# Fifteen products for eighteen in w1, and layernorm 1 of the next image by halves beside fc2

## The chip, the core and the metric

The kernel runs on one core of one Trainium2 chip. A core has a matrix engine (TensorE, PE in the profile), three engines for elementwise work (VectorE or DVE, ScalarE or ACT, GpSimd or POOL), a queue engine (SyncE or SP) and 16 DMA engines; they run side by side and wait for each other by semaphores. TensorE writes to PSUM banks (128 partitions by 512 float32), the others read them from there. The metric is the device time of one execution in microseconds, lower is better. Everything is computed in float32.

## The reference

Eight images of 384 channels by 32 by 32 pixels pass through a transformer block and then a ConvNeXt block. Cut to what matters here:

```python
# layer 0, per image, 1024 tokens of 384 channels
xn = layernorm(xf, g1, beta1)                       # layernorm 1
qkv = einsum('bnc,oc->bno', xn, w_qkv) + b_qkv
...                                                 # attention with 8 heads of 48, projection
x1 = out + shortcut
xn2 = layernorm(x1, g2, beta2)                      # layernorm 2
h = gelu(einsum('bnc,oc->bno', xn2, w_fc1) + b_fc1) # 384 -> 1536
y = x1 + einsum('bnh,oh->bno', h, w_fc2) + b_fc2    # 1536 -> 384
# layer 1
y = depthwise_conv7x7(x) + dw_b
y = layernorm(y) * ln_w + ln_b                      # layernorm 3
y = gelu(einsum('bhwc,cd->bhwd', y, w1) + b1)       # 384 -> 1536
gx = sqrt(sum(y * y, axis=(1, 2)))
y = grn_gamma * (y * gx / (mean(gx) + eps)) + grn_beta + y
y = einsum('bhwd,dc->bhwc', y, w2) + b2             # 1536 -> 384
out = x + y
```

## The kernel before

Channels lie on the partitions: an image is a tile of 128 partitions by 3 by 1024 (CT is 3, N is 1024, NH is 512, half an image). Images are counted from 0 to 7. A product is one matmul of a 128 by 128 block of weights with 512 tokens.

**Stages.** The loop at L1759 goes through the images. For image b it runs q and k, attention, fc1 for the first half of the tokens and then the second (`mlp`, L882), and fc2 (`by_thirds`, L908). Then it ends layer 1 of image b-1: w1 (`grn_up`, L1124), the values of image b+1 (`next_values`, L1730), w2 (`grn_down`). The depthwise convolution of image b runs on DVE beside these stages (`convolution`, L1061), with some taps made by ACT and added by POOL's DMA (`help_convolution`, L1092). Image 7 and the last layernorms have a path of their own.

**Fewer products.** fc2, w2 and q/k use a scheme in which a matrix cut in 3 by 3 blocks times one cut in 3 by 2 takes 15 products and not 18: some sums of the weight blocks are made once, in image 0, and kept in DRAM (`sums_singly`, L1370, for q/k), some sums of the token blocks are made for each image (`thirds_of`, L388), and the results are combined by DVE and ACT (`tiles_by_thirds`, L406, with the tables SINGLY, BANKS and SUMS). w1 uses another: for a pair of output tiles, 11 products instead of 12, with four differences of token blocks (`block_differences`, L1115) in the tile `attn` and weight sums in `s_w1`.

**The planner.** Work that is not TensorE's own is written as generators. `Flow` (L136) counts the products issued, each as 0.857 us; a generator says how long it wants to wait, and its next step is issued at the first product end after that. `after(first, chain)` asks every 1.0 us whether another chain has ended, `finish` issues the rest of a chain at once. The planner only decides in which order instructions stand in the five engines' programs; each engine then runs its own in order.

**Layernorms.** `layernorm` (L485) takes half an image: two adds over the three channel tiles (L499, L502), a sum over the partitions by TensorE, subtraction (L509), squares on ACT (L516), two adds (L520, L523), again a sum, Ln and Exp on ACT, and three multiplications (L537). Where a half is folded (`token_sums`, L459), POOL's DMA first adds one half of the partitions to the other (L474), and TensorE sums on one half of its rows only (L480):

```python
nc.gpsimd.dma_start(out=t[rows[j], cols], in_=t[rows[1 - j], cols], accum_op=ALU.add)
yield wait
...
for i in rows:
    nc.tensor.matmul(out=total[i, :], lhsT=ones[rows[j], :64], rhs=t[rows[j], cols], start=True, stop=True)
```

`abreast` (L549) runs the two halves of an image step by step beside each other, one folded to the upper rows and one to the lower. Layernorm 3 (`conv_norm`, L1696) and layernorm 1 of the next image (`next_norms`, L1706) are such pairs. The second comes 50 us after the end of fc1, behind layernorm 3; it falls into w1. The image for it is loaded at the end of fc1, because the tile `xn` has one buffer, which layernorm 2 also writes for fc1.

**Queues.** SP's queue holds the loads of weights (nine ring buffers, `Weights`, L283), of images and the small transfers of attention. POOL's holds the folds, the helped taps and the accumulating DMAs of fc2 and w2 (`adding`, L949, and `difference`, L866).

Of the kernel before, what the change touches and what calls it, by code (L numbers as in the profile page):

```python
# [51 lines left out]
P = 128  # L52
# [123 lines left out]
def block_kernel(  # L176
# [10 lines left out]
    w1: bass.AP,  # L187
    w2: bass.AP,
# [20 lines left out]
    s_w1 = dram.tile([P, HT // 2, 4, P], F32, tag="s_w1", bufs=1, name="s_w1")  # L209
# [7 lines left out]
    def load_x(b, tag, parts=2, engine=nc.sync):  # L217
        xt = one.tile([P, CT, N], F32, tag=tag, name=f"{tag}_{b}")
        src = image_of(x, b).rearrange("(c p) n -> p c n", p=P)
        for i in range(parts):  # L220
            cols = slice(i * N // parts, (i + 1) * N // parts)
            engine.dma_start(out=xt[:, :, cols], in_=src[:, :, cols])
        return xt

    vec = const.tile([P, NVEC], F32, name="vec")
    wqkv = const.tile([P, 3 * CT * C], F32, name="wqkv")
    wqk_sb = wqkv[:, : 2 * CT * C].rearrange("p (c m o) -> p c m o", c=CT, o=P)
    wv_sb = wqkv[:, 2 * CT * C :].rearrange("p (c o) -> p c o", c=CT)
    wproj_sb = const.tile([P, CT, C], F32, name="wproj_sb")
    ident = const.tile([P, P], F32, name="ident")  # L230
# [9 lines left out]
    third_e = const.tile([P, NH], F32, name="third_e")  # L240
# [112 lines left out]
    def plan_w1(tag, fast=True):  # L353
        plan = []
        for i in range(NC):
            plan.append(((f"w1_{tag}", i, "A"), chunk(w1, i)))
            if fast:
                plan.append(((f"w1_{tag}", i, "S"), s_w1[:, i, :, :].rearrange("p j o -> p (j o)")))
        return plan
# [28 lines left out]
    def thirds_of(src, places, e):  # L388

        b11, b12, b21, b22, b31, b32 = (src[:, s, half(n)] for s in range(CT) for n in range(2))  # L390
        f, h, e2, g, f2, h2, g2, f3, d = places
# [12 lines left out]
        return steps, (b12, b21, e, b22, f, h, e2, g, b31, f2, h2, g2, f3, b32, d)  # L404

# [138 lines left out]
    def weight_places(name):  # L544

        tiles = [three.tile([P, 2, NH], F32, tag="p", name=f"{name}_{i}") for i in range(2)]
        return [t[:, j, :] for t in tiles for j in range(2)]

# [30 lines left out]

    def qk(b, xn, weights=None):  # L580
# [3 lines left out]
        big = one.tile([P, HT * N], F32, tag="big", name=f"qk_{b}")  # L584
        parts = big[:, : 2 * NP * N].rearrange("p (i m n) -> p i m n", i=2, m=NP)
        if b == 0:
            spare_sums.append(big[:, 2 * NP * N :])
# [148 lines left out]
    def attention(b, xt, qT, kT, last_tile, ready, first):  # L736
# [44 lines left out]
        for n in range(len(steps) + 2):  # L781
# [10 lines left out]
            if n - 2 == len(steps) // 2 + 6:  # L792
                for chain in first:
                    flow.finish(chain)
                xn = one.tile([P, CT, N], F32, tag="xn", name=f"xn2_{b}")
# [20 lines left out]
    def exact_attention(xt, qT, kT):  # L816

        nc.vector.memset(attn, 0.0)
        for qt in range(N // P):
# [295 lines left out]
    def block_differences(acc):  # L1115

        b11, b12, b21, b22 = (acc[:, s, half(n)] for s in range(2) for n in range(2))
        t1, t2, t3, t4 = (attn[:, i, :] for i in range(4))
        yield 3.0
        for dst, one_, other in ((t1, b12, b11), (t2, b22, t1), (t3, b22, b12), (t4, b21, t2)):  # L1120
            nc.vector.tensor_tensor(dst, one_, other, ALU.subtract)
            yield 1.2

    def grn_up(b, acc, weights, tag):  # L1124
# [5 lines left out]
        b11, b12, b21, b22, b31, b32 = (acc[:, s, half(n)] for s in range(CT) for n in range(2))  # L1130
        t1, t2, t3, t4 = (attn[:, i, :] for i in range(4))
        wa = f"w1_{tag}"
        spent = {}

        def finish(m):
            other_table(y[:, m, :], y[:, m, :], AF.Gelu, bias=b1[:, m : m + 1])

        def squares(i):
            for m in (i, i + HT // 2):
                waste = spent[i].rearrange("p a n -> p (a n)")  # L1140
                nc.scalar.activation(waste, y[:, m, :], AF.Square, accum_out=gx[:, m : m + 1])

        for i in range(HT // 2):
            j = i + HT // 2
            raw, sums = weights.at(wa, i, "A"), weights.at(wa, i, "S")
            a11, a12, a13, a22, a23 = (raw[:, k, :] for k in range(5))
            s1, s2, s3, s4 = (sums[:, k, :] for k in range(4))
            spent[i] = ps_s.tile([P, 2, NH], F32, tag="s", name=f"h_{b}_{i}_5")
            p5 = spent[i][:, 0, :]
            c11, c12, c21, c22 = (y[:, m, half(n)] for m in (i, j) for n in range(2))  # L1150

            def product(*pairs):
                bank = o_tile(f"h_{b}_{i}")
                accumulate(bank, list(pairs))
                return bank

            def plus(dst, bank, part):
                nc.vector.tensor_tensor(dst, bank, part, ALU.add)  # L1158

            nc.scalar.copy(c21, product((a11, b11)))  # L1160
            if i:
                finish(j - 1)
                squares(i - 1)
            plus(c11, product((a13, b31), (a12, b21)), c21)
            accumulate(p5, [(s1, t1)])
            plus(c21, product((s2, t2)), c21)
            plus(c12, p5, c21)
            plus(c12, product((s4, b22), (a13, b32)), c12)
            finish(i)
            plus(c21, product((s3, t3)), c21)  # L1170
            plus(c22, p5, c21)
            plus(c21, product((a23, b31), (a22, t4)), c21)
# [791 lines left out]
```

## Time and profile before

| | us |
|---|---|
| three runs | 3286.0, 3287.73, 3288.41; median 3287.73 |
| the profiled execution | 3286.43, its span 3284.5 |
| granted TensorE clock, mean | 0.996 |
| start of fc2, w1 and values of image 3 | 1359.4, 1413.3, 1472.6 |

The page gives busy time of each engine over the whole span; its stages differ, so the parts are read from the order of time of one image. Lines that begin with a line number are groups of instructions: engine, operation, tiles, shapes, count, busy time and mean of one. A mean of 592 ns for a matmul of 512 columns is the length of one of its two passes, which overlap; the distance from one product to the next is what counts. Such rows of the page are:

```profile
L444 PE MATMUL h<-acc,w_A 128*128 128x512 f32 x432 | 207.4, 596 | 0.0
L1158 DVE TENSOR_TENSOR y<-h,y 128x512 f32<-128x512 f32 x288 | 198.1, 690 | 93.6 <-PE h L444 80.4
hid<-hid POOLq DMA_DIRECT2D x42, 512.0 KB, 7.9
```

The first is part of w1's products, in two passes each; the second the adds by which w1's results are combined, 48 for an image; the third the accumulating DMAs of fc2 with the median time from issue to landing.

### The profile page before, as it was taken

The page shows a single profiled execution, that of the slowest core. Times are in us where ns is not written, and L with a number is a line of the kernel's source. Part 1 is how long each engine was busy: PE and PEld are TensorE (multiplying, and loading weights), DVE is VectorE, ACT ScalarE, POOL GpSimd, SP SyncE. Part 2 cuts the span into 40 slices and gives each one's busy share as a digit, 9 for nine tenths or more (in the row PEclk, how much of TensorE's full clock was granted, in tenths as well). Part 3 has the DMA queues.
Part 4 walks back from the last instruction along what each step waited for, and adds up shares of the span by engine and source line. Part 5 has one row for each costly group of instructions (what it writes and reads, how often), then busy time and mean ns, then how long its engine had stood idle before and what let it go on. Part 6 is the DMA issues. An engine that isn't in the chain of part 4 may idle for free. (4 is left out here: it accounts for less than half of the span.)

```text
span 3284.5 us, 38862 instructions
## 1 busy us (share of the span) xinstructions
PE 3262.0 (99%) x14288; PEld 1410.0 (43%) x14288; DVE 2413.3 (73%) x3220; ACT 1630.0 (50%) x2243; POOL 481.8 (15%) x567
## 2 busy tenths in 40 slices
PE   9999999999999999999999999999999999999999
PEld 5334444443344434444334443444434444444455
DVE  4444787787867878678786787867887788879850
ACT  3542763447634375353762646526474365723631
POOL 2111210112110121101211012110221112200000
PEclk9999999999999999999999999999999999999999
DMA  6336733647345563536536374273843637433231
GB/s 236 115 109 146 166 61 78 154 111 171 60 97 144 135 139 58 127 116 169 102 61 140 106 188 82 56 169 87 202 74 61 179 88 189 74 79 85 68 91 54
DMA packets 202160, 380.08 MB, mean 116 GB/s; under 512 B 41072, under 2 KB 47088, under 8 KB 201328
## 3 DMA queue, kind: packets, MB, share of 16 engines
q0 software_dynamic: 80928, 161.78, 26.7%
q1 hardware_dynamic: 120752, 215.09, 21.3%
q8 instruction: 114, 1.87, 0.2%
q10 hardware_dynamic: 288, 0.71, 0.1%
q14 instruction: 78, 0.64, 0.1%
HBM read 197.25 MB, written 35.78 MB: 71 GB/s over the span
## 5 line engine op out<-in xcount | busy, mean ns | idle before, releaser
L1087 DVE SCALAR_TENSOR_TENSOR acc<-pad,vec,acc 128x870 f32<-128x870 f32 (+8 forms) x861 | 963.1, 1154 | 7.0 <-DMA acc<-tap 1.7
L756 ACT ACTIVATE p<-s 128x1024 f32<-128x1024 f32 x512 | 524.4, 1024 | 267.0 <-PE s L747 260.2
L747 PE MATMUL s<-qk 48*64 48x512 f32 x4096 | 537.9, 592 | 0.7 <-ACT qk L593 0.7
L767 PE MATMUL o<-p,v 64*64 64x512 f32 x4096 | 534.5, 589 | 0.0
L384 PE MATMUL fc<-xn,fc 128*128 128x512 f32 x1152 | 502.6, 595 | 2.0 <-DVE acc L509 2.0
L1109 POOL DMA_DIRECT2D acc<-tap x294 | 253.4, 868 | 1184.5 <-ACT tap L1108 698.6
L384 PEld LDWEIGHTS fc<-xn,fc 128*128 128x128 f32 x1152 | 218.6, 190 | 282.0 <-issue 271.6
L444 PE MATMUL fc_p<-hid,fc 128*128 128x512 f32 x728 | 319.3, 594 | 0.0
L456 ACT ACTIVATE hid<-fc,bfc_f 128x512 f32<-128x512 f32 x192 | 131.4, 686 | 339.8 <-PE fc L384 339.7
L767 PEld LDWEIGHTS o<-p,v 64*64 64x64 f32 x4096 | 162.2, 133 | 278.7 <-issue 272.8
L747 PEld LDWEIGHTS s<-qk 48*64 48x64 f32 x4096 | 158.4, 133 | 278.1 <-issue 225.9
L444 PE MATMUL o_p<-y,w 128*128 128x512 f32 x624 | 270.9, 592 | 0.0
L1158 DVE TENSOR_TENSOR y<-h,y 128x512 f32<-128x512 f32 x288 | 198.1, 690 | 93.6 <-PE h L444 80.4
L1108 ACT ACTIVATE tap<-pad,vec 128x512 f32<-128x512 f32 x294 | 215.9, 735 | 1.4 <-DMA acc<-tap 1.2
L444 PEld LDWEIGHTS fc_p<-hid,fc 128*128 128x128 f32 x728 | 137.4, 190 | 178.7 <-issue 174.9
L444 PE MATMUL h<-acc,w_A 128*128 128x512 f32 x432 | 207.4, 596 | 0.0
L444 PEld LDWEIGHTS o_p<-y,w 128*128 128x128 f32 x624 | 118.0, 190 | 148.7 <-issue 134.9
L1087 DVE SCALAR_TENSOR_TENSOR wqkv<-pad,vec,wqkv 128x377 f32<-128x377 f32 (+24 forms) x288 | 177.3, 686 | 0.6
L876 ACT COPY pad<-x 128x512 f32<-128x512 f32 x48 | 30.2, 635 | 253.6 <-DVE x L942 196.6
L708 DVE TENSOR_TENSOR attn<-o,attn 128x512 f32<-128x512 f32 x64 | 44.1, 689 | 152.1 <-ACT attn L706 152.1
L689 PE MATMUL proj<-attn,wproj_sb 128*128 128x512 f32 x288 | 127.3, 595 | 1.1 <-DVE attn L734 1.1
L444 PEld LDWEIGHTS h<-acc,w_A 128*128 128x128 f32 x432 | 80.6, 190 | 109.0 <-issue 93.4
(361 smaller groups left out, 3822.8 us busy)
## 6 DMA issues: line engine op xcount, KB each, us to landing
acc<-tap POOLq DMA_DIRECT2D x294, 256.0 KB, 3.6
w_A<-in_w SPq DMA_DIRECT2D x72, 384.0 KB, 3.3
fc<-s_fc SPq DMA_DIRECT2D x91, 256.0 KB, 4.3
hid<-hid POOLq DMA_DIRECT2D x42, 512.0 KB, 7.9
fc<-in_wfc SPq DMA_DIRECT2D x54, 384.0 KB, 4.2
w<-s_w SPq DMA_DIRECT2D x78, 256.0 KB, 2.6
y<-y POOLq DMA_DIRECT2D x36, 512.0 KB, 7.1
qk<-s_qk SPq DMA_DIRECT2D x42, 320.0 KB, 5.0
```

The lines of the kernel that those rows point to most:

```text
L384: nc.tensor.matmul(out=ps, lhsT=lhsT(k), rhs=rhs(k)[:, half(h)], start=(k == 0), stop=(k == nk - 1))
L444: nc.tensor.matmul(out=bank, lhsT=lhsT, rhs=rhs, start=k == 0, stop=k == len(pairs) - 1)
L456: nc.scalar.activation(dst, src, function, **kw)
L689: nc.tensor.matmul(out=ps, lhsT=wproj_sb[:, m, ct * P : (ct + 1) * P], rhs=attn[:, m, :], start=(m == 0), stop=(m == CT - 1),)
L708: nc.vector.tensor_tensor(attn[:, m, :], outs[1], attn[:, m, :], ALU.add)
L747: nc.tensor.matmul(out=s[64 * i : 64 * i + 64, j, :], lhsT=kT[64 * j : 64 * j + HD, m, k0 : k0 + 64], rhs=qT[64 * j : 64 * j + HD, m, half ...
L756: nc.scalar.activation(p, s, AF.Exp)
L767: nc.tensor.matmul(out=outs[i][64 * j : 64 * j + 64, :], lhsT=v[keys, t, at : at + 64], rhs=p[keys, j, :], start=(t == 0), stop=(t == KT - 1),
L1087: nc.vector.scalar_tensor_tensor(dst, window, tap, dst, ALU.mult, ALU.add)
L1108: nc.scalar.mul(t.rearrange("p (h w) -> p h w", w=W), window, tap)
L1109: nc.gpsimd.dma_start(out=acc[:, ct, half(h)], in_=t, accum_op=ALU.add)
L1158: nc.vector.tensor_tensor(dst, bank, part, ALU.add)
```

## The change

Five things are changed.

1. w1 is computed by `tiles_by_thirds`, in four groups of 15 products for 3 output tiles each. Its weight sums are made in image 0 from a new input `w1t`, with those of q/k, by two chains that go through one group at a time (`sums_for_tiles`), and its token sums by ten differences (`make_thirds`) in place of four.
2. The tile `xn` has two buffers. One takes the next image, loaded in the middle of attention (`next_image`); the other holds layernorm 2's output for fc1 and then six of the token sums, of w1 first and of q/k later (`before_fc2`).
3. From image 2 to image 6 the rest of the convolution is issued when layernorm 2 ends, and layernorm 3 starts 16 us later (`end_soon`).
4. Layernorm 1 of the next image no longer comes after layernorm 3 as a pair. Its halves run one after the other (`halves_of_next`), from 24 us after layernorm 2 (1 us in image 1), with the tiles `res` for their sums; in image 0 it stays a pair.
5. To make room, wqk no longer has a place of its own (it is loaded into the big tile of q and k), and `ident`, `third_e` and w1's old sums are gone; the last image's convolution is kept in an `xn` buffer.

```diff
-        xt = one.tile([P, CT, N], F32, tag=tag, name=f"{tag}_{b}")
+        xt = one.tile([P, CT, N], F32, tag=tag, bufs=2 if tag == "xn" else 1, name=f"{tag}_{b}")
...
-    def thirds_of(src, places, e):
+    def thirds_of(src, spare):
...
-        f, h, e2, g, f2, h2, g2, f3, d = places
+        f, h, e2, g = averages()
+        e, f2, h2, g2, f3, d = (spare[:, s, half(n)] for s in range(CT) for n in range(2))
...
+    def make_thirds(what, src, us, spare):
+        steps, thirds[what] = thirds_of(src, spare)
+        for step in steps:
+            nc.vector.tensor_tensor(*step)
+            yield us
...
+                next_image(b)
                 for m in (NP - 1, *range(CT)):
                     flow.finish(chains[0, m])
...
+        def gelu(g, r):
+            m = g + 4 * (r - 1)
             other_table(y[:, m, :], y[:, m, :], AF.Gelu, bias=b1[:, m : m + 1])
...
+        def square(g, r):
+            m = g + 4 * (r - 1)
+            nc.scalar.activation(waste, y[:, m, :], AF.Square, accum_out=gx[:, m : m + 1])
+
+        for g in range(HT // CT):
+            tiles = {}
...
+            def behind(n):
+                if g and n == 3:
+                    gelu(g - 1, 2)
+                    gelu(g - 1, 1)
+                elif g and n == 1:
+                    square(g - 1, 2)
+                elif g and n == 4:
+                    square(g - 1, 1)
+                elif n == 14:
+                    gelu(g, 3)
+                elif n == 7:
+                    square(g, 3)
+
+            c = {f"c{r + 1}{n + 1}": y[:, g + 4 * r, half(n)] for r in range(CT) for n in range(2)}
+            for _ in tiles_by_thirds(weights, f"w1_{tag}", g, thirds["w1"], c, bank, behind):
+                pass
+        for what in (gelu, square):
+            for r in (2, 1):
+                what(g, r)
...
         def conv_norm(b, ln):
-            if b > 0:
+            if b == 0:
+                xn = state["xn"]
+                norm = abreast(xn, xn, eps0, "g1", "ln1_1", True, gentle=True)
+                state["norm1"] = flow.spawn(after(ln, norm))
+            else:
                 acc = state["acc"]
                 how = dict(wait=5.0) if b < B - 1 else dict(wait=3.4, factor=2.4)
                 norm = abreast(acc, acc, eps1, "lnw", f"ln3_{b - 1}", True, **how)
-                if b < B - 1:
-                    norm = sequence(norm, block_differences(acc))
-                state["norm3"] = flow.spawn(after(ln, after(state["help"], after(state["conv"], norm))))
-
-        def next_norms(b):
+                if 1 < b < B - 1:
+                    state["norm3"] = flow.spawn(after(ln, sequence(end_soon(b), norm)))
+                    state["norm1"] = flow.spawn(after(ln, halves_of_next(b, 24.0)))
+                else:
+                    state["norm3"] = flow.spawn(after(ln, after(state["help"], after(state["conv"], norm))))
+                if b == 1:
+                    state["norm1"] = flow.spawn(after(ln, halves_of_next(b, 1.0)))
...
+        def sums_for_tiles(i):
+            width = len(FORMS) * P
+            spare = large[0][:, (2 * NP + 2 * i) * N : (2 * NP + 2 * i + 2) * N]
+            for w, store, g in ((wqkt, s_qk, i), (w1t, s_w1, i), (w1t, s_w1, i + 2)):
+                yield from sums_singly(w[:, g * width : (g + 1) * width], store[:, g : g + 1], spare)
+                yield 8.0
...
+        def end_soon(b):
+            end_convolution(b)
+            yield 16.0
...
+        def halves_of_next(b, us):
+            yield us
+            xn = state["xn"]
+            for h in range(2):
                 name = f"ln1_{b + 1}"
-                places = (lambda: weight_places(name)) if b else averages
-                norm = abreast(xn, xn, eps0, "g1", name, True, places=places, gentle=b > 0, factor=1.4 if b else 1.7)
-                state["norm1"] = flow.spawn(after(state["norm3"], norm, 50 if b else 11))
...
+                places = lambda: res_places(f"{name}_{h}")
+                yield from layernorm(xn, xn, h, eps0, "g1", name, True, spare=places, fold=h, wait=5.0, gentle=True)
+
+        def before_fc2(b):
+
+            end_convolution(b)
+            spare = state["spare"] = one.tile([P, CT, N], F32, tag="xn", bufs=2, name=f"thirds_{b}")
+            if b > 0:
+                state["w1"] = flow.spawn(after(state["norm3"], make_thirds("w1", state["acc"], 1.4, spare)))
...
             if b < B - 1:
-                y, gx = grn_up(b - 1, acc, weights, b - 1)
+                flow.finish(state["w1"])
+                flow.finish(state["norm1"])
+                y, gx = grn_up(b - 1, weights, b - 1)
```

## The prediction

> **What bounds the kernel now.** I read the page first (busy shares, slices), then TensorE's waits, then the order of time of one image (number 3 of 0 to 7, 1140 to 1538 us; numbers 2 to 6 repeat it with a period of 398 us), and last how long DMAs take to land.
>
> ```profile
> PE 3262.0 (99%) x14288; PEld 1410.0 (43%) x14288; DVE 2413.3 (73%) x3220; ACT 1630.0 (50%) x2243; POOL 481.8 (15%) x567
> DVE  4444787787867878678786787867887788879850
> ```
>
> TensorE (PE) is busy 99% of the span: what the change takes from it is time, and what it makes it wait is time. VectorE (DVE) is at 73%, but unevenly. Of the waits of PE two rows matter:
>
> ```profile
> PE ln_var L480 <- DMA ln_sq<-ln_sq: 2.5, 3, 1.3
> PE ln_sum L480 <- DMA ln_a<-ln_a: 1.9, 1, 1.9
> ```
>
> So 4.4 us go to folded layernorm sums whose DMA was late, all in the first two images; from 900 to 2800 us PE waits 1.1 us in all, and for no fold. What a product and a sum cost is read from the w1 stage in PE's order of time (start, length, instructions):
>
> ```profile
> 1419.32 1.02 PE L444 MATMUL h<-attn,w_S 128*128 128x512 f32 x2
> 1420.17 1.02 PE L444 MATMUL h<-acc,w_A 128*128 128x512 f32 x2
> 1421.03 1.02 PE L444 MATMUL h<-attn,w_A 128*128 128x512 f32 x2
> 1421.98 0.65 PE L480 MATMUL ln_sum<-ln_a,ones 64*64 64x512 f32 x2
> 1422.00 0.65 PE L480 MATMUL ln_sum<-ln,ones 64*64 64x512 f32 x2
> 1422.46 0.59 PE L480 MATMUL ln_sum<-ln_a,ones 64*64 64x512 f32 x2
> 1422.48 0.60 PE L480 MATMUL ln_sum<-ln,ones 64*64 64x512 f32 x2
> 1423.00 3.89 PE L444 MATMUL h<-acc,w_A 128*128 128x512 f32 x8
> ```
>
> From start to start a product takes 0.858 us (the groups' mean of 1.02 counts an overlap). The sums of *both* halves of layernorm 1 run beside each other, on different quarters of the array: 1423.00 - 1421.03 - 0.86 = 1.11 us for the two together.
>
> In fc2 of this image (1359.4 to 1413.3) DVE runs in bursts:
>
> ```profile
> 1386.72 2.35 DVE L942 TENSOR_TENSOR hid<-hid 128x1024 f32<-128x1024 f32 x2
> 1388.99 0.74 DVE L939 SCALAR_TENSOR_TENSOR x<-fc_p,vec,x 128x512 f32<-128x512 f32 x1
> 1389.65 0.74 DVE L939 SCALAR_TENSOR_TENSOR x<-fc_n,vec,x 128x512 f32<-128x512 f32 x1
> 1390.31 0.68 DVE L942 TENSOR_TENSOR fc_spare<-fc_n,fc_spare 128x512 f32<-128x512 f32 x1
> 1391.03 0.69 DVE L942 TENSOR_TENSOR x<-fc_spare,x 128x512 f32<-128x512 f32 x1
> 1391.63 0.68 DVE L942 TENSOR_TENSOR fc_spare<-fc_spare 128x512 f32<-128x512 f32 x1
> 1392.35 0.69 DVE L942 TENSOR_TENSOR x<-fc_spare,x 128x512 f32<-128x512 f32 x1
> ```
>
> This is what is issued at once after the seventh of the fifteen products of fc2 (four matmuls each): 6.9 us with the add before it (1386.1 to 1393.0), in which nothing else gets through. A fold in its turn is a 128 KB accumulating DMA on POOL. Behind two 512 KB ones of fc2 (image 1, issues from 581 to 587 us; then image 3, where nothing was ahead of it):
>
> ```profile
> hid<-hid POOLq DMA_DIRECT2D x2, 512.0 KB, 7.8
> ln_sq<-ln_sq POOLq DMA_DIRECT2D x1, 128.0 KB, 9.4
> attn<-attn POOLq DMA_DIRECT2D x1, 128.0 KB, 9.8
> ```
> ```profile
> ln_sq<-ln_sq POOLq DMA_DIRECT2D x1, 128.0 KB, 3.7
> ```
>
> 9.4 us against 3.7 from issue to landing. The reader should keep three things: PE full, DVE lumpy in fc2, a fold slow behind the adds.
>
> [...]
>
> **The change part by part.** The working is against the profiled run, 3286.43 us (span 3284.5 and 1.9 around it, 1.3 under the median of 3287.73).
>
> *w1.* Six images (0 to 5) go through it. Before: six pairs of 11 matmuls, 66; after: four groups of 15, 60. 36 matmuls by 0.858 = **-30.9 us**. Their rate stays 0.858 if DVE and ACT keep up. The same form runs in q/k without a wait of PE. For w1, by slots of 0.858 (a group is 12.9): DVE has 11 adds of 0.63 to 0.69, 7.6 us; ACT 5 copies of 0.58, 3 gelus of 1.05 to 1.15 and 3 squares of 1.2, 9.9 us. The tightest return is bank n: slot 12's two subtractions end at 12.6, the next group wants it at 12.9. Slot 5 wants the add of slot 2 (ends 3.4, wanted 4.3); slot 8 the copy of slot 5 (5.9, wanted 6.9). Taken at nothing; if 0.5 us per group is lost, +12. Weights are 12 loads of 320 KB for 6 of 384 and 6 of 256: 3.84 MB both times. The tail on ACT is two gelus and two squares for one and two: about 0.5 us later at a matmul (gxsum) with 1.9 us to spare.
>
> *Layernorm 1 by halves.* For six images (2 to 7) the sums of the two halves no longer stand beside each other. One half alone still takes both passes, and image 1 shows halves that came apart (594.10, 595.02, 596.03) at 0.92 and 1.01. So four times 1.1 for two times 1.1: **+13.2 us** (10.8 at 1.0 each; no gain is possible, since each stands alone in PE's order).
>
> *Where the steps fall.* The planner runs a step at the first product end after its wait, and a product counts 0.857: 0.8 is one product, 1.2 two, 1.8 three, 2.6 four, 5.0 six, 16 nineteen, 24 twenty-nine. (Checked on before: layernorm 3 from sum to variance, 2+2+3+3+9 = 19 products and a sum, 17.4 us; traced 1361.18 to 1378.71, 17.5.) Images 2 to 6: layernorm 2's variance stands 48 products ahead of fc2 (1317.32), it ends at -43; layernorm 3 begins near -23, so its first sum moves from behind fc2's second product to -9.5, into fc1, where DVE sat idle 21.4 us before L509. That part is well hidden. Layernorm 1 begins at -13 and needs 43 products per half; with some 3 products that the sums themselves count, half 1's first add falls at 27.5 and the second at 29.5, on the two sides of fc2's burst at 28.
>
> *The ledger there* (us from the start of fc2; two sums of 1.1 lie before it). DVE has, new in fc2, ten w1 differences of 0.6 (before: four) and layernorm 1's last three multiplies of half 0 and ten operations of half 1; with fc2's own 33 us and the end of layernorm 3, about 53 of 56 us. The backlog ahead of the burst is some 1.3 us: the first add runs at 26.9, the burst from 27.6 to 34.4, a difference, and the second add ends at 35.6. The fold is issued at 35.7. fc2's adds into g were issued at 28.7 and 30.4 (1388.03 and 1389.74 before); in images 0 and 1 the fold landed 9.9 and 10.1 us after the second of such a pair: 40.3. By itself it would land 3.3 after issue, 39.0. PE reaches the sum ten products after the second add's step, 39.5 products, 36.2 us. It stands 2.8 to 6; I take 3.9, with fc2 behind it. The variance comes last in fc2: its second add is behind the six adds after the thirteenth product (3.8 us), its fold lands 8.2 us after that product, PE is there at 6.9: 1.3 (0.9 to 2.5). Five images by 5.2: **+26 us** (16 to 42).
>
> *Image 1* has the convolution in the way, layernorm 3 in fc2 as before, and half 1's variance behind the same adds: fold issued near 33.7, landing about 42, wanted at 36.4; **+5.5** (2.4 to 9).
>
> *Image 0.* Layernorm 1 moves from fc2 to fc1: its two waits (1.89 and 0.33) go, something of POOL's preparation may meet it: **-1** (-2.2 to +5). Sums of w1 are now 72 operations of 128 columns for 4 of 768, and q/k's 36 for 18, some 20 us of DVE at 4 tenths in this stage; their loads are 960 KB on POOL (the 1920 KB one took 16 us), beside attention. Taken in that range.
>
> *Edits with one answer.* The image's load (2 by 768 KB, 6.7 us) moves on SP from fc2 to mid-attention, behind the last reciprocals' broadcasts of its half (due 11 products after the pair's end; the load stands 14 after it), so nothing urgent queues behind it; a late fold of layernorm 2 would cost 1 us. The second buffer's owner was read out by then. wqk in the big tile, the missing identity, the last image's place: nothing.
>
> Sum: -30.9 + 13.2 + 26 + 5.5 - 1 = +12.8: 3299 for the profiled run, **3300** against the median.
>
> **The rivals.** *Faster* (0.17): the second add of half 1 runs ahead of the burst. It decides at one or two products: at 27.5 instead of 29.5 its fold is issued at 28 to 29, lands before 36, and no sum waits. Then -30.9 + 13.2 - 1 = -18.7, 3269. For it: layernorm 3 in fc2 never waited in images 2 to 6. Against it: the rounding reproduced before's order. *DVE is the bound of fc2* (0.14): 53 of 56 us leave no room; if the operations take 0.66 for 0.63 the seventh product waits for e (ledger: 23.5, wanted 24.5) and later ones too, some 5 us more in five images: 3325. Against it: PE never waited at 48 of 54 us. *The w1 stage does not keep its rate* (0.05): +12, 3312. My own case has 0.64, its own range is 3287 to 3322.
>
> **How the numbers follow.** Under 0.2% (6.6 us) a measurement of this kernel cannot tell from no change. Slower: 0.51 of my 0.64 (the rest lies at the low ends of the waits), 0.14 and 0.05, 0.70. Same: 0.13 and 0.02 of the faster case, 0.15. Faster: 0.15. The range reaches down into the faster case and up to the third: 3273 to 3326.
>
> **What would show it.** Right: w1 at 0.858 without waits; L480's sums alone at 1.1 us; waits of PE at ln_sum and ln_var on a fold, 4 to 6 us in each fc2 from image 1 to 6, and DVE's L502 behind L939/L942. Wrong: no such waits; waits at products of fc2 on DVE; or waits in w1 on ACT.

## The result and the profile after

| | before | after |
|---|---|---|
| median us (runs) | 3287.16 (4) | 3319.30 (4) |
| lowest to highest us | 3286.00 to 3288.41 | 3318.39 to 3322.16 |
| ratio, 95% interval | | 1.0099, 1.0082 to 1.0117 |
| span of the profiled run, us | 3284.5 | 3316.9 |
| mean granted clock of TensorE | 0.996 | 0.991 |

The change makes the kernel 32 us slower. The forecast was 3300 us, in a range of 3273 to 3326. The line numbers of the kernel after differ: products of thirds are L416, their additions L432, products of fc2 L445, folded sums L481, the fold's DMA L475, the two additions ahead of a fold L500 and L503, fc2's additions on VectorE L950 and L953.

The first view is the page of the kernel after: busy time, share and instructions of each engine, then VectorE's busy tenths in 40 slices.

```profile
PE 3260.0 (98%) x14216; PEld 1408.2 (42%) x14216; DVE 2431.7 (73%) x3318; ACT 1666.4 (50%) x2319; POOL 480.7 (14%) x567
...
DVE  4644788787876878768787687866877778879850
```

TensorE has 72 instructions less (36 products, two passes each) and is busy 2 us less, yet the span is 32 us longer. The busy time of a stretch in which instructions overlap is counted once. A busy sum that hardly falls while work was taken away says that the same instructions took longer, or overlap less (as the sums of layernorm 1's halves do now). Next, the waits of TensorE after (waiting line and what ended the wait: us in all, times, longest).

```profile
PE ln_sum L481 <- DVE hid L953: 12.7, 3, 4.3
PE ln_var L481 <- DMA ln<-ln: 8.9, 6, 3.5
PE ln_sum L481 <- DMA ln<-ln: 7.9, 2, 4.0
PE b L273 <- DVE w_gbeta L1511: 5.6, 1, 5.6
...
PE h_n L416 <- ACT y L437: 1.9, 1, 1.9
```

The first and third rows are the same stand: the first sum of layernorm 1's second half, five times about 4.1 us, once in each of images 2 to 6. (VectorE's L953 is named where it ended within the same moment; the fold's DMA is the releaser that belongs to the sum.) The second row is that half's variance, 3.5 us in image 1 and about 1.1 us in each of images 2 to 6. The fourth is new too: a stand of 5.6 us in image 0. The last is all that TensorE waits for in w1.

To see where time went I took the start of the first matmul of each stage from TensorE's order of time in both traces:

| us, start to start | before | after | difference |
|---|---|---|---|
| image 0, all | 312.3 | 319.0 | +6.7 |
| image 1, all | 401.3 | 404.8 | +3.4 |
| images 2 to 6, each: fc1 (in most; without the projection that stands in it) | 63.6 | 66.05 | +2.4 |
| fc2 | 53.9 | 63.3 to 64.5 | +9.4 to +10.5 |
| w1 | 59.3 | 51.6 | -7.7 |
| images 2 to 6, all stages, sum | 1988.5 | 2012.0 | +23.5 |
| the rest | | | -1.3 |

All other stages of images 2 to 6 agree within 0.1 us in most images. So the loss is in fc2 and in image 0, and 2.4 us an image in fc1.

In fc2 of image 3, which starts at 1376.83, VectorE's order of time shows the burst and what stands behind it (start, length, operation):

```profile
1404.86 2.35 DVE L953 TENSOR_TENSOR hid<-hid 128x1024 f32<-128x1024 f32 x2
...
1410.49 0.69 DVE L953 TENSOR_TENSOR x<-fc_spare,x 128x512 f32<-128x512 f32 x1
1411.10 0.69 DVE L404 TENSOR_TENSOR attn<-acc,attn 128x512 f32<-128x512 f32 x1
1411.70 0.69 DVE L503 TENSOR_TENSOR ln<-ln,xn 128x512 f32<-128x512 f32 x1
```

The second addition of half 1 (L503) ends 35.6 us after the stage's start. GpSimd's order of time shows that its fold goes out behind fc2's two accumulating transfers:

```profile
1405.46 1.19 POOL L965 DMA_DIRECT2D hid<-hid  x1 [3.73 <-PE fc_p L445]
1407.18 1.19 POOL L965 DMA_DIRECT2D hid<-hid  x1 [0.53 <-PE fc_p L445]
1412.94 0.85 POOL L475 DMA_DIRECT2D ln<-ln  x1 [4.57 <-DVE ln L503]
```

From issue to landing this fold took 4.9 us and the variance's, at 1436.37, 2.7. TensorE, which is done with its products at 1413.7, stands for the first, and the next 40 matmuls of fc2 start behind its sum, at 1419.29 (in brackets the idle time before the row and its releaser):

```profile
1403.28 10.46 PE L445 MATMUL fc_p<-hid,fc 128*128 128x512 f32 x24
1418.02 1.34 PE L481 MATMUL ln_sum<-ln,ones 64*64 64x512 f32 x4 [4.28 <-DVE hid L953]
1419.29 18.82 PE L445 MATMUL fc_p<-hid,fc 128*128 128x512 f32 x40
1439.17 1.07 PE L481 MATMUL ln_var<-ln,ones 64*64 64x512 f32 x4 [1.06 <-DMA ln<-ln]
```

The sum itself took 1.34 us; the variance, the same four matmuls, took 1.07. What is behind that is seen in windows of the same stretch (window of time: its length; busy time and instructions of PE, PEld, DVE, ACT, POOL; then PEclk, the granted clock; DMA share; GB/s):

```profile
1413.00:1418.00 5.00, 0.74 (x2) 0.01 (x1) 4.88 (x7) 0.00 (x0) 0.79 (x1) 1.00 0.86 213
1418.00:1420.50 2.50, 2.48 (x6) 0.91 (x7) 1.10 (x2) 0.00 (x0) 0.00 (x0) 0.64 0.02 7
1420.50:1423.00 2.50, 2.50 (x6) 0.99 (x5) 1.32 (x2) 0.00 (x0) 0.00 (x0) 0.68 0.00 0
1423.00:1426.00 3.00, 3.00 (x9) 1.33 (x8) 1.59 (x3) 0.00 (x0) 0.00 (x0) 1.00 0.17 29
...
1418.75:1422.10 3.35, 3.35 (x6) 1.27 (x5) 2.42 (x3) 0.00 (x0) 0.00 (x0) 0.50 0.02 5
```

The 0.64 and 0.68 are means: as the last row shows, the clock is at 0.50 from 1418.7 to 1422.1, and at 1.00 before and after. So a stand of 4.3 us costs more than 4.3 us. Image 0 shows the same behind its stand of 5.57 us; these are TensorE's rows there, attention's score and value matmuls:

```profile
118.76 0.56 PE L273 MATMUL b<-ones,w_gbeta 128*128 128x1 f32 x2 [5.57 <-DVE w_gbeta L1511]
119.24 1.98 PE L755 MATMUL s<-qk 48*64 48x512 f32 x8
121.00 1.93 PE L775 MATMUL o<-p,v 64*64 64x512 f32 x8
...
125.59 1.03 PE L755 MATMUL s<-qk 48*64 48x512 f32 x8
```

The same eight matmuls take 1.98 us right after the stand and 1.03 some 7 us later; the clock is at 0.50 from 118.2 to 125.0.

In the five fc2 stages of images 2 to 6 the trace has the clock at 0.50 for 3.4, 3.4, 6.8, 6.8 and 6.8 us, 27.3 us in all. TensorE is at work in 24.3 us of them. If its matmuls take twice as long there, as in image 0 (1.98 us for 1.03), half of that, some 12 us, is lost; this is an estimate.

The stretches at 0.50 last 3.4 us or a multiple of it: 3.4 and 6.8 us in fc2, 10.2 us once near the end (3193.6 to 3203.9). TensorE need not be wholly idle ahead of one: in image 3 the 3.4 us just before the fall (1415.3 to 1418.7) hold 0.7 us of matmuls. A later run goes further. The prediction priced no such thing.

### The profile page after: what moved, and what is told of

Same layout as the page of the kernel before. It is cut to its first block, busy times and chain, and to the rows that moved or that the text cites. A ratio compares the mean times of both kernels' runs of the same rounds, so it can differ in the third digit from the quotient of the medians.

```text
span 3316.9 us, 38888 instructions
## 1 busy us (share of the span) xinstructions
PE 3260.0 (98%) x14216; PEld 1408.2 (42%) x14216; DVE 2431.7 (73%) x3318; ACT 1666.4 (50%) x2319; POOL 480.7 (14%) x567
## 5 line engine op out<-in xcount | busy, mean ns | idle before, releaser
L755 PE MATMUL s<-qk 48*64 48x512 f32 x4096 | 548.1, 593 | 0.2 <-ACT qk L601 0.2
L775 PE MATMUL o<-p,v 64*64 64x512 f32 x4096 | 545.6, 591 | 0.0
L445 PE MATMUL fc_p<-hid,fc 128*128 128x512 f32 x728 | 330.8, 611 | 0.0
L445 PE MATMUL o_p<-y,w 128*128 128x512 f32 x624 | 270.9, 592 | 0.0
L445 PEld LDWEIGHTS fc_p<-hid,fc 128*128 128x128 f32 x728 | 141.5, 196 | 189.3 <-issue 185.4
L445 PEld LDWEIGHTS o_p<-y,w 128*128 128x128 f32 x624 | 118.0, 190 | 148.7 <-issue 134.9
L1098 DVE SCALAR_TENSOR_TENSOR acc_last<-pad,vec,acc_last 128x377 f32<-128x377 f32 (+24 forms) x288 | 177.3, 690 | 0.6
L675 PE MATMUL v<-wv_sb,xn 128*128 128x384 f32 x384 | 126.8, 487 | 0.0
L432 DVE TENSOR_TENSOR y<-h_n,y 128x512 f32<-128x512 f32 x72 | 49.8, 692 | 71.3 <-PE h_n L416 68.8
L675 PEld LDWEIGHTS v<-wv_sb,xn 128*128 128x128 f32 x384 | 72.5, 190 | 50.1 <-issue 3.3
```

Source lines behind the costliest of these rows:

```text
L445: nc.tensor.matmul(out=bank, lhsT=lhsT, rhs=rhs, start=k == 0, stop=k == len(pairs) - 1)
L675: nc.tensor.matmul(out=ps[:, :C], lhsT=xn[:, k, t * P : (t + 1) * P], rhs=wv_sb[:, k, :], start=(k == 0), stop=(k == CT - 1),)
L755: nc.tensor.matmul(out=s[64 * i : 64 * i + 64, j, :], lhsT=kT[64 * j : 64 * j + HD, m, k0 : k0 + 64], rhs=qT[64 * j : 64 * j + HD, m, half ...
L775: nc.tensor.matmul(out=outs[i][64 * j : 64 * j + 64, :], lhsT=v[keys, t, at : at + 64], rhs=p[keys, j, :], start=(t == 0), stop=(t == KT - 1),
L1098: nc.vector.scalar_tensor_tensor(dst, window, tap, dst, ALU.mult, ALU.add)
```

## The experiments

Two questions were open. Is the loss in fc2 a late fold and the clock after it, or is VectorE the bound of fc2, so that any wait taken away comes back under another name? And what makes image 0 longer?

| kernel | us, median (runs) | ratio to before, 95% interval |
|---|---|---|
| after | 3319.3 (4) | 1.0099, 1.0082 to 1.0117 |
| after, earlier halves | 3287.4 (12) | 0.9998, 0.9989 to 1.0007 |
| after, unfolded half sums | 3281.5 (20) | 0.9976, 0.9969 to 0.9983 |
| after, later column sum in image 0 | 3319.1 (4) | 1.0099, 1.0082 to 1.0117 |
| before, early sums in w1 | 3345.8 (4) | 1.0178, 1.0161 to 1.0195 |
| before, sums less early | 3335.4 (4) | 1.0150, 1.0129 to 1.0171 |
| after, w1's weight sums in image 1 | 3322.3 (4) | 1.0103, 1.0086 to 1.0120 |
| after, layernorm 1 as a pair in w1 | 3303.0 (4) | 1.0044, 1.0027 to 1.0061 |
| both of the last two | 3302.7 (4) | 1.0046, 1.0029 to 1.0062 |
| unfolded, weight sums paced | 3281.4 (13) | 0.9983, 0.9974 to 0.9991 |
| after, no VectorE work on w1's tiles | 3320.3 (4) | 1.0096, 1.0079 to 1.0113 |
| unfolded, weight sums in three places | 3283.4 (17) | 0.9986, 0.9979 to 0.9994 |
| after, w1's tiles moved by a fifteenth | 3321.3 (4) | 1.0096, 1.0079 to 1.0113 |

**More room for the fold.**

```diff
-        totals = yield from token_sums(a, f"{name}_sum{h}", fold, wait)
+        totals = yield from token_sums(a, f"{name}_sum{h}", fold, wait + room)
...
-  state["norm1"] = flow.spawn(after(ln, halves_of_next(b, 24.0)))
+  state["norm1"] = flow.spawn(after(ln, halves_of_next(b, 18.0)))
...
-  yield from layernorm(xn, xn, h, ..., fold=h, wait=5.0, gentle=True)
+  yield from layernorm(xn, xn, h, ..., fold=h, wait=5.0, gentle=True, room=5.0 * h)
```

> The kernel after, but layernorm 1's halves start 6 us earlier in fc2 and the sum of half 1 is entered 5 us later. Theory (a late fold: TensorE stands about 4 us for the first sum of half 1, then runs some us at about half the clock): in images 1 to 6 the waits on the fold fall from 12.7 us (three of 4.3) and 7.9 us (two of 4.0) to under 2 us each in sum, fc2 shrinks by 5 to 8 us in each, and the time is 3319 - 40 = 3279 us, 3275 to 3295. Rival (VectorE is the bound of fc2, so that whatever waits there only changes its name): other waits of the same length appear in fc2, which stays at 63 to 64 us, and the time stays at 3312 to 3322 us.

Measured: 3287.4 us, 32 less than after. In its trace the second addition of half 1 in image 3 runs at 1398.37, ahead of the burst at 1401.62. From 900 to 2900 us TensorE waits for the half sums no more than this, and none of it in fc2, where it is busy all of the time (waits in that window; in image 3 it is half 0's sum in fc1, and so is the second row in image 2):

```profile
PE ln_sum L481 <- DMA ln<-ln: 1.8, 4, 0.9
...
PE ln_sum L481 <- ACT ln_sq L517: 1.4, 1, 1.4
```

fc2 of images 2 to 6 takes 56.2 us in place of 63.3 to 64.5. VectorE has the same operations there, and in fc2 no wait took the place of the one removed: VectorE is not the bound of fc2, and that rival falls. That the shrink is 7.1 to 8.2 us where the two stands together were 5.3 shows what the clock costs: in the five images fc2 shrinks by 38.5 us, 26.0 of it stands, and the 12.5 left are the some 12 us of half clock worked out above.

**No fold at all.** The half sums multiply all 128 rows by ones; the transfer and what waits for it go.

```diff
-  yield from layernorm(xn, xn, h, ..., fold=h, wait=5.0, gentle=True)
+  yield from layernorm(xn, xn, h, ..., fold=None, wait=5.0, gentle=True, still=True)
...
+        if still:
+            yield wait
         totals = yield from token_sums(a, ...)
```

> The kernel after, but the sums of layernorm 1's halves run over all 128 rows, with no addition of the upper half's rows and no transfer for them; they are entered after the same waits as before. Theory (a late fold): with no transfer to wait for, the stands of 4 us at the first sum of half 1 go, and the clock stays near 1.0 there; a sum of three products may take less or more than the folded one's 1.11 us, by under 1 us per image in all. Time 3319 - 45 = 3274 us, 3265 to 3290. Rival (VectorE is the bound of fc2): only four small transfers go, VectorE loses two operations of some 0.7 us per half, fc2 stays at over 62 us, time 3310 to 3320 us.

Measured: 3281.5 us; fc2 of images 2 to 6 takes 55.3 us, and no wait on a sum of layernorm 1's halves is left from 900 to 2900 us. A lone half costs less unfolded, as TensorE's rows of image 3 show:

```profile
1405.51 1.02 PE L467 MATMUL ln_sum<-ln,ones 128*128 128x512 f32 x2
1406.37 17.33 PE L445 MATMUL fc_p<-hid,fc 128*128 128x512 f32 x40
1423.54 1.02 PE L467 MATMUL ln_var<-ln,ones 128*128 128x512 f32 x2
1424.39 1.02 PE L416 MATMUL h_n<-attn,w 128*128 128x512 f32 x2
```

From its start to the next product's the variance takes 0.85 us, like any product; folded, in the kernel after, it took 1.01 (1439.17 to 1440.18). In the kernel before a folded pair ran side by side and took 1.11 us, where two lone unfolded halves take 1.70; a half alone gains nothing by the fold. This kernel is faster than both, than before by 0.24% (0.17 to 0.31). Both times are in the theory's ranges but 8 us above its values. Not for want of gain in fc2, which gave back 43.6 us in the first kernel and 50.7 in the second, image 1 counted in: w1 became longer, by 0.8 and 1.0 us an image and by 1.7 and 4.3 in image 1; there were new short stands in images 2, 3 and 6; and in the second image 0 took 322.8 us for 319.0. Image 0's instructions are the same in both and in the kernel after, so the 319.0, 319.6 and 322.8 us show how much one profile of image 0 can differ from another: some 4 us.

**The price of a stand, in the kernel before.** The same instructions, only the folded sums of layernorm 1 are entered too early in w1.

```diff
-        yield 2.6 * slow
+        yield 0.1 if gentle else 2.6 * slow
         totals = yield from token_sums(a, ...)
...
-  norm = abreast(xn, xn, ..., gentle=b > 0, factor=1.4 if b else 1.7)
+  norm = abreast(xn, xn, ..., gentle=b > 0, factor=1.4 if b else 1.7, wait=0.6 if b else 3.4)
```

> The kernel before, with the same instructions, but the folded sums of the next layernorm 1 are entered too early in w1 in six images, so that TensorE stands some 3 to 4 us for the first and about 1 us for the second, with nothing else of it changed. Theory (a stand of 4 us costs itself and some us at about half the clock after it): 3287 + 6 x (3.7 + 1 + 2.7) = 3331 us, 3322 to 3340, and the windows after each stand show a granted clock of 0.5 to 0.7. Rival (the stand costs only itself, and the low clock of the kernel after has to do with the crowd in fc2): 3287 + 6 x 4.7 = 3315 us, 3308 to 3319, with the clock at 0.99 behind the stands.

Measured: 3345.8 us, 57 above the runs of before beside it (3288.6), more than either theory allowed. w1 takes 68.1 to 69.8 us for 59.3 to 59.6. TensorE's rows of image 2, then windows of the same stretch:

```profile
1027.76 1.02 PE L444 MATMUL h<-acc,w_A 128*128 128x512 f32 x2
1032.59 1.46 PE L480 MATMUL ln_sum<-ln_a,ones 64*64 64x512 f32 x4 [3.81 <-DMA ln_a<-ln_a]
1034.71 1.97 PE L480 MATMUL ln_sum<-ln,ones 64*64 64x512 f32 x4 [0.67 <-DMA ln<-ln]
1036.62 3.64 PE L444 MATMUL h<-acc,w_A 128*128 128x512 f32 x4
```

```profile
1032.50:1036.70 4.20, 3.44 (x9) 0.63 (x9) 0.69 (x1) 0.00 (x0) 0.00 (x0) 0.58 0.93 355
1036.70:1039.00 2.30, 2.30 (x3) 1.09 (x4) 0.69 (x1) 0.00 (x0) 0.00 (x0) 0.50 0.05 14
1039.00:1041.00 2.00, 2.00 (x5) 0.77 (x4) 0.65 (x2) 0.00 (x0) 0.00 (x0) 0.76 0.87 283
```

TensorE stands 4.5 us and w1 grows by 9.4. The clock is at 0.50 from 1033.2 to 1040.0; TensorE works 6.2 us in there, and by the same estimate half of that, 3.1 us, is lost. The 1.8 us left are not the clock: the two halves now come apart, and their sums, which took 1.11 us side by side, take some 2 us one after the other. In this kernel nothing crowds fc2, and without these stands the kernel before has the clock at 1.00 in the same stage (1016 to 1074 us), so here the low clock goes with the stand itself. The theory is right in kind. Its price of 2.7 us was too low, and the halves coming apart it left out. In the six images the clock is low for 6.8 or 10.2 us (its mean over the run is 0.990, for 0.996 before), in the kernel after for 3.4 or 6.8; why it is once, twice or three times 3.4 us was not tried.

**A shorter stand.** The same edit with `wait=1.9` for 0.6.

> The kernel before with its folded sums in w1 too early by less: TensorE should stand about 2 us, in place of 3.7, for the first sum in each of six images. Theory (behind a stand the clock falls only from some length on, between 1.6 us, where the kernels before and after mostly show none, and 3.6 us): if 2 us is short of it, w1 takes 59.3 + 2.5 = 62 us and the time is 3287 + 6 x 2.5 = 3302 us, 3298 to 3306. Rival (any stand brings it): w1 takes 65 to 68 us, time 3320 to 3335 us.

Measured: 3335.4 us (3328.4 to 3342.2), at the top of the rival's range: w1 takes 64.9 to 68.3 us. The trace is of the fastest of the four executions. The single stands were mostly about 1 us, not 2, but two stood close together. Windows of image 3, in which TensorE idles 0.93 us before the first sum (1433.52) and 1.20 before the second (1435.79), and of image 4, in which it idles 1.02 and 0.64 us:

```profile
1433.50:1435.60 2.10, 1.08 (x4) 0.21 (x4) 0.00 (x0) 0.00 (x0) 0.00 (x0) 1.00 1.03 350
1435.70:1438.00 2.30, 2.21 (x5) 0.63 (x6) 0.00 (x0) 0.00 (x0) 0.00 (x0) 0.50 0.82 335
1438.00:1440.00 2.00, 2.00 (x3) 0.86 (x3) 0.20 (x1) 0.00 (x0) 0.00 (x0) 0.50 0.19 31
...
1838.50:1841.90 3.40, 2.22 (x7) 0.41 (x5) 0.69 (x1) 1.47 (x2) 0.00 (x0) 1.00 1.04 277
1841.90:1845.30 3.40, 2.91 (x9) 1.18 (x10) 0.71 (x2) 0.00 (x0) 0.00 (x0) 1.00 0.84 342
```

In image 3 the clock is at half behind the second stand, from 1435.7 to 1442.5. Two stands of 2.1 us in all within 3.4 us were enough. In image 4 it stays at 1.00, as it does in image 5 after 0.93 and 0.82 us. So not any stand brings it, and there the theory was right; w1 takes 64.9 us in those two images all the same, because TensorE waits for VectorE and ScalarE there too (0.7 us at a time) and the halves come apart. An unbroken idle stretch was not needed. One stand of 1.89 us, ahead of 292.96 in image 0 of the kernel before, was followed by the half clock too (294.1 to 297.5). From which share of idle time on it happens, these runs don't say.

**Layernorm 1 back in w1, as a pair.** Fifteen products and layernorm 3's place stay; the pair's sums take attention's PSUM tiles.

```diff
-  state["norm1"] = flow.spawn(after(ln, halves_of_next(b, 24.0)))
...
+  norm = abreast(xn, xn, eps0, "g1", name, True, places=lambda: pair_places(name), gentle=True)
+  state["norm1"] = flow.spawn(after(state["w1"], norm, 50))
...
-  total = o_tile(f"{name}_{j}")[:, : cols.stop - cols.start]
+  total = sum_tile(f"{name}_{j}")[:, : cols.stop - cols.start]
```

> The kernel after, but layernorm 1 of the next image is again made as a pair of halves side by side in w1, as in the kernel before, with its sums in the PSUM tiles that attention uses; fifteen products, thirds and the place of layernorm 3 stay as they are after. Theory (the loss lies in the halves in fc2, their four lone sums and their late folds, and fifteen products need no help from them): a period of images 2 to 6 is 397.4 - 6 x 0.858 = 392.3 us, image 1 takes 396, image 0 keeps its 6.7 us, time 3260 us, 3252 to 3270. Rival (w1 by fifteen holds its 0.858 us only because layernorm 1 is out of it: its additions on VectorE stand behind the layernorm's): w1 takes 58 to 62 us instead of 54, time 3275 to 3310 us.

Measured: 3303.0 us; the rival is right. w1 takes 59.3 us in images 2 to 6 (2.2 of them the pair's sums), not 54, and TensorE's waits over the whole run begin with three rows that the kernel after doesn't have at this size:

```profile
PE h_z L416 <- ACT y L437: 12.3, 10, 1.6
PE h_n L416 <- ACT y L437: 7.7, 3, 3.7
PE h_x L416 <- DVE y L432: 7.5, 10, 0.7
```

With layernorm 1 in the stage, ScalarE's copies and VectorE's additions come too late for the PSUM tiles that the products want back. The w1 stage keeps 0.858 us a product only because layernorm 1, in this arrangement, has left it.

**Image 0.** First, the stand of 5.57 us alone: its column sum is entered later (`yield 14.0` for `4.0` in the shift through w2).

> The kernel after, but TensorE's column sum for the shift through w2 is entered 10 us later in image 0's attention. Theory (w1's sums now stand before w_gbeta's operations on VectorE, and each of them waits there for its transfer, so that TensorE comes to the column sum 5.6 us too early): the wait of 5.57 us goes, and with it the low clock after it; attention of image 0 falls from 132.3 to about 125 us and the time to 3312 us, 3309 to 3315. Rival (image 0's attention is held up by VectorE's and the transfers' crowd as a whole): the wait comes at another place, attention stays at 130 to 133 us and the time at 3317 to 3322 us.

Measured: 3319.1 us. That stand went, and another came, 6.2 us at proj for attention's scaled rows; image 0 takes 319.4 us. The rival holds.

Then w1's four weight sums moved as a whole to image 1's attention, alone and with the pair in w1.

```diff
-  for w, store, g in ((wqkt, s_qk, i), (w1t, s_w1, i), (w1t, s_w1, i + 2)):
+  parts = ((w1t, s_w1, i), (w1t, s_w1, i + 2)) if b else ((wqkt, s_qk, i),)
+  for w, store, g in parts:
...
+  if b == 1:
+      singly = [flow.spawn(after(None, sums_for_tiles(1, i), 20 + 10 * i)) for i in range(2)]
```

> The kernel after, but the four sums of w1's tiles are made in image 1's attention, not in image 0's; the two of the q and k weights stay where they are. Theory (image 0 is longer by 6.7 us because VectorE stands there in order for the transfers of w1's tiles, and the transfers crowd): image 0 goes back from 319.0 to 312 to 314 us, image 1's attention has room for them and stays at 112.6 to 113.5 us, and the time is 3313 us, 3310 to 3316. Rival (the same work costs as much wherever it stands): image 1 lengthens by what image 0 wins, and the time stays at 3317 to 3322 us.

> Both of the other two edits: layernorm 1 as a pair in w1, and w1's weight sums in image 1's attention. If the two losses are separate they add up: 6 us below the pair alone, 3254 us, 3246 to 3264. If image 0's loss is not in w1's sums, or if w1's tile sums hold up image 1, it is the same as the pair alone within 2 us.

Measured: 3322.3 and 3302.7 us, nothing gained. Image 0 does go back, to 312.4 and 309.4 us, but image 1 grows by 11.0 and 11.4 us. In the first of the two kernels TensorE's waits in image 1's attention are these:

```profile
PE proj L697 <- DVE attn L742: 6.6, 1, 6.6
PE proj L697 <- DVE x L705: 2.0, 1, 2.0
```

So most of image 0's loss is w1's weight sums, and it goes where they go. How much is seen from the start of q and k to the first product of fc1: 165.2 us before; 178.1 to 181.8 in the kernel after and in five others that make all the sums there at the same pace or only carry their tiles; 171.5 and 168.5 in the two kernels just measured. The 3 to 6 us that these two still lose against before come from something else (the load of the next image and the loads for q and k moved into this stretch too), which no run separates. In the whole of image 0 they are hidden, because fc1 and fc2 became 6.2 us shorter.

Which part of w1's sums is it? One kernel leaves VectorE's operations on the tiles out (18 for each set, 72 in all; the expectation counts 15), loads and stores staying:

```diff
+  if store.shape[1] == 1 and w_is_w1:
+      yield 4.8
+  else:
       plus(r[6], r[6], a12)
...
```

> The kernel after, with VectorE's 15 operations on each of w1's four sets of tiles left out, so that the tiles are carried to the chip and back unsummed and w1 multiplies by wrong weights; loads, stores and all else stay. Theory (image 0's loss comes from VectorE: 60 operations, some 12 us, and the stands in order before them): image 0 takes 312 to 314 us in place of 319.0, the time is 3313 us, 3309 to 3316. Rival (the 7.7 MB of transfers crowd out attention's small ones): image 0 stays at 318 to 320 us and the time at 3317 to 3322 us.

Measured: 3320.3 us, image 0 321.5, and 180.7 us up to fc1. VectorE's operations are not it; the transfers alone cost as much. That they crowd attention's small transfers is an assumption (in the trace SyncE issues the small ones and GpSimd w1's). The busy share of the DMA engines fits it as far as it goes: from 110 to 150 us it is 0.54 after and 0.30 and 0.34 in the two kernels with the sums moved to image 1. But attention's small transfers by way of the tensor `back` took not much longer to land, 2.3 us in the median after and 2.0 before (longest 6.3 and 4.9), so how the large ones hold attention up is not shown.

Two milder arrangements, on the kernel without folds: more time between load and first operation (`yield 13.0` for `9.0`, and `3.0` for `8.0` behind each set); and the four sets spread over image 0's attention (two), its fc2 and image 1's attention (one each).

> The kernel with unfolded half sums (3281.5 us), and in image 0 the first operation on each set of weight tiles is entered 13 us of TensorE's work behind its load, not 9, with the pause behind each set cut from 8 to 3 us. Theory (VectorE stands in order for the load of w1's tiles, and what is queued behind it, the scaling of attention's rows and w_gbeta, is late for TensorE): VectorE's waits on the loads, 5.6 us and 5.4 us in the kernels seen, fall below 2 us, image 0 shrinks from 322.8 to 312 to 316 us and the time to 3273 us, 3269 to 3277. Rival (not the standing but the operations and transfers themselves fill that stretch): image 0 stays at 318 us or more and the time at 3278 to 3284 us.

> The kernel with unfolded half sums (3281.5 us), with the four sets of w1's tiles summed in three places: two in image 0's attention, one in image 0's fc2 (in the buffer that the thirds take later), one in image 1's attention. Theory (attention's small transfers wait behind the sets' large ones, and what matters is how much of them falls into the 110 us of one attention): with half of the traffic image 0 falls from 319 to 322 us to 311 to 315 us, one set in image 1 costs it under 2 us, and the time is 3274 us, 3269 to 3278. Rival (each set costs its 1.5 to 3 us wherever it stands, as moving all four to image 1 did): time 3279 to 3284 us.

Measured: 3281.4 and 3283.4 us, both in their rivals' ranges; image 0 takes 318.8 and 323.6. In the first VectorE's wait for w1's tiles and the stand at w_gbeta are gone, but a late fold of layernorm 2 (4.0 us) and some short stands have their place. Two sets in image 0's attention cost no less than four (181.6 us up to fc1).

Last, the same transfers at a fifteenth of their bytes, w1's store being filled later:

```diff
+  part = 1 if few else shape[2]
-  nc.gpsimd.dma_start(out=t, in_=w.rearrange(...))
+  nc.gpsimd.dma_start(out=t[:, :, :part], in_=w.rearrange(...)[:, :, :part])
...
-  nc.gpsimd.dma_start(out=store, in_=t)
+  nc.gpsimd.dma_start(out=store[:, :, :part], in_=t[:, :, :part])
```

> The kernel after, but in image 0's attention the four loads and four stores of w1's tiles carry one block of fifteen each (64 KB for 960), with the same number of transfers in the same place of GpSimd's queue and the same operations on VectorE; w1's store is filled afterwards, in image 0's fc1, by four plain stores of 960 KB, so that w1 multiplies by wrong weights. Theory (the bytes crowd attention's small transfers): image 0's q/k weights and attention through proj fall from 186 to 174 to 177 us, image 0 from 319 to 309 to 314 us, the time to 3308 to 3315 us. Rival (the places in GpSimd's queue and on VectorE hold, not the bytes): that stretch stays at 183 to 190 us and the time at 3316 to 3323 us.

Measured: 3321.3 us, image 0 318.1: the rival by its number. But the four plain stores did not go out in fc1, as the expectation has it; they went out at 192.6 us, in attention's tail, and TensorE's waits from 30 to 290 us are:

```profile
PE proj L697 <- DVE attn L742: 4.3, 1, 4.3
PE ln_sum L481 <- DMA ln_a<-ln_a: 2.1, 1, 2.1
```

The first stands at 217.3 us, behind the stores, in the second projection; up to there only the second is left, and nothing at w_gbeta. From the start of q and k to the first product of fc1 this kernel takes 170.1 us, 8.0 less than after and as much as the kernels without these sums (171.5 and 168.5), although it has the same number of transfers and the same operations on VectorE. So the stand moved with the bytes, which points to the bytes and not to the places in the queue. It is one profile, and it doesn't say why two sets cost as much as four.

## Why the prediction was right, and where not

The direction, the range and the mechanism of the late fold held; the sum was short by 19.5 us (forecast +12.8, measured +32.3 between the two profiled runs). That the range held is in part luck: its upper end was set by longer waits and by VectorE as the bound of fc2, not by the clock, nor by an image 0 this long.

- *w1, -30.9.* Right. The stage takes 51.60 us, 60 times 0.858 being 51.5. "Taken at nothing" for VectorE and ScalarE was right too, apart from 1.9 us in image 1; the pair in w1 shows that it hung on layernorm 1 leaving, which the prediction doesn't say.
- *Sums alone, +13.2.* Right within 0.1 us a sum: 1.01 from start to start for the half alone in image 3, 1.07 by the row; fc1 grew by 2.4 us for one sum of layernorm 3 and one of layernorm 1. That "no gain is possible" was wrong: it holds for folded sums, and unfolded a lone one takes 0.85.
- *The ledger of fc2.* Right nearly to the row: second addition ends 35.6 us after the stage's start, as forecast, fold issued 36.1 (35.7), stand 3.9 to 4.3 (3.9), variance 1.1 (1.3). The ten stands add up to 26.0 us, the forecast +26. One entry was off: VectorE was to be busy 53 of 56 us in fc2. It is busy 48.4 of 63.4 in image 3, and 47.0 of 56.2 once the stands are gone; the rival of VectorE as the bound rested on the 53.
- *"Five images by 5.2: +26 us".* This is the term that was mis-sized. fc2 grew by 49.9 us in the five images: 26.0 in stands, 10.8 in two more sums each, and 13.1 that the forecast didn't have. Some 12 of these are the half clock behind the stands, so the term is +39. Early sums in the kernel before show the same low clock (0.50 from 1033.2 to 1040.0 in image 2), where nothing crowds fc2.
- *Image 1, +5.5* with its products and sums: forecast +2.6 in all, measured +3.4. Right by its number, with luck in it: the stand was 3.5 us and not 5.5, and the clock, low for 6.8 us behind it, cost an estimated 3.4 more (half of that time).
- *Image 0: "-1 (-2.2 to +5)".* This step failed: +6.7. The two waits that it let go did go, but w1's weight sums, which were "taken in that range", cost TensorE a stand of 5.6 us and the clock after it. Up to fc1 image 0 took 12.9 us longer than before, 7 to 10 of them for these sums by the runs that move them or thin them, and fc1 and fc2 gave 6.2 back. (A stand of 1.9 us for a fold of layernorm 2 is new too, but it is there without w1's sums as well, 2.2 us.) The runs tie the loss to the sums' transfers and not to VectorE's operations on them, and the last one to their bytes; how these hold attention up, and why half of them cost as much, stays open.
- *The rivals.* VectorE as the bound of fc2 falls with the first two experiments. The faster one, the addition and its fold ahead of the burst, is what the first experiment made: 3287 us, not 3269, because image 0 kept its loss and images 2 to 6 won 1.1 us each on average, not 3.0. The loss of w1's rate is real, but only with layernorm 1 in the stage.

The expected gain of 31 us is thus in the profile, in w1, and is given back in three places: four lone sums per image for two pairs, stands in fc2 with the clock behind them, and image 0.

## What to carry to other kernels

Where TensorE is the bound, price a stand of it at its length and the slow stretch behind it; in the kernel after a stand of 3.5 to 5.6 us came with 3.4 or 6.8 us at half clock, which cost an estimated 1.7 to 3.4 us more (half of TensorE's busy time in it). When a step is moved beside a stage that runs in bursts, give its wait room from the moment its operand can be ready behind the burst, or drop the transfer that it waits for: a half that no longer ran beside its twin gained nothing from a fold here (1.01 us folded, 0.85 unfolded). Large preparing transfers beside a stage with small urgent ones cost TensorE time in either of the two stages tried here (7 to 10 us in attention of image 0; image 1 grew by 11.0 and 11.4 us with them), and spreading them over more stages won nothing (3283.4 us for 3281.5).

## What the runs showed that was not expected

- With a stand of 3.5 to 5.6 us in a long busy kernel TensorE's clock was at 0.50 for 3.4, 6.8 or 10.2 us, and its matmuls took up to twice as long (1.97 us for 1.08, 1.98 for 1.03). Two stands of 0.93 and 1.20 us within 3.4 us did the same, and one of 1.89 us; 0.93 and 0.82 us, and 1.02 and 0.64, did not.
- The sum of a lone half over 128 rows cost 0.85 us from start to start, folded to 64 rows 1.01.
